# Second attention of a four-layer graph network: four row buffers, seven slots per period, ScalarE's passes and copies in a fixed alternation, results one period later

## The chip, the cores and the metric

The kernel runs on one core of one Trainium2 chip. A core has five engines that work side by side and wait for one another through semaphores: TensorE (matrix products; PE in the profile, PEld for its weight loads), VectorE (DVE), ScalarE (ACT), GpSimd (POOL) and SyncE (SP, which here only starts DMAs). Each engine takes its own instructions strictly in the order in which the program has them. The metric is device time in microseconds (us) of one execution.

## The reference

Four layers on 3327 nodes with 256 features, each `x = layernorm(x + layer(x, adj))`. Layer 0 averages over neighbours, layer 1 is a graph convolution with a state-space scan, layer 2 is graph attention, layer 3 is top-p attention with diffusion. The change touches layer 3, whose core is:

```python
def _top_p_attention(X, W1, W2, W3):
    q = X @ W1.T @ W2.T
    k = X @ W3.T
    probs = softmax(q @ k.T, axis=-1)
    idx = argsort(-probs, axis=-1)
    sp = take_along_axis(probs, idx, axis=-1)
    cs = cumsum(sp, axis=-1)
    keep_sorted = cs - sp < TOP_P            # 0.9
    ...
    A = probs * mask
    return A / maximum(A.sum(-1, keepdims=True), 1e-12)

R = (S + eye(N)); R = R / R.sum(-1, keepdims=True)
for n in range(2):
    A = _top_p_attention(Xa, W1, W2, W3)
    Xf = R @ Xf
    Xa = A @ Xa
    Z = Z + Xf @ U1[n].T + Xa @ U2[n].T
h = layernorm(X + Z)
```

In each of the two steps every row of the attention keeps the largest probabilities until their sum reaches 0.9. `S` is the adjacency.

## The kernel before

Rows are padded to 3328 and cut into 26 tiles (`nt`) of 128 rows. A tile's row of attention, `e`, is 128 x 3328 numbers. Layer 3 runs two stages over the tiles, the first attention (step 0, `p=0`) and the second attention (step 1, `p=1`), which is the last work of the kernel.

Helpers are Python generators: each `yield` is a point where the loop that drives them may go on to another one. The loop therefore writes down the order of work by hand, and a scheduler behind it orders each engine's instructions by readiness, except those wrapped in `keep_in_program_order` (`here`), which stay in the order in which the loop wrote them. For a tile of the second attention the helpers are:

- `scores` (L781): products of queries and keys in four groups of two 416-wide halves into one PSUM tile `sc`; ScalarE copies each group into `e` (L795, the last group in two pieces, L798).
- `search_long` (L903): finds the cut-off value of each row. `m8` (L913) takes a maximum of the first 416 columns. ScalarE then makes six passes over the whole of `e`: Exp of half the value for a sum (L917), Exp in place (L918), and, after VectorE has set a first threshold `c1` (L922 to L928), Relu and Sign about it (L929, L931). From these VectorE estimates a second threshold `c2` (L933 to L949), and ScalarE passes again (L950, L952). A third threshold `c3` (L965 to L974) cuts `e` into `z` (L977, 3328 wide), of whose 26 segments VectorE takes the top eight each (L853, MAX8), ranks them in six rounds (L864, L866) and finds the crossing `v` (L873 to L876). Ties are dropped by two MATCH_REPLACE8 (L1001), and the select L1008 clears everything under `v` and sums what is kept.
- `attended` (L830): seven groups of four transposes of `e` into PSUM (`tp`, four buffers), a copy of each group by ScalarE (`wt`, L839), four products each with `G` (L841).
- `diffused` (L814) and `aggregated` (L801): 26 products (L809) of the adjacency, loaded in chunks of `J3` = 7 tiles by SyncE (`at`, L807, three buffers), and the result `xf` (L827). It is made `DL` = 4 tiles ahead of the attention that uses it.
- `second` (L1049): two normalizations of the row (`h`, L1052, L1060, L1061; statistics L84, L85). GpSimd computes the inverse root (`power`, L593, L594), VectorE `nb` (L1068), ScalarE the last scaling (L1069), SyncE writes `out` (L1071).

The driving loop (L1146) has one round per tile i. It works on four things: the attention of tile i-1 (`values`), the search of tiles i and i+1, and the scores of tile i+2; the result of tile i-1 follows in the same round. `e` has three buffers (L1109), so the scores of tile i+2 go into the buffer from which tile i-1 has just been transposed.

`J3`, `DL`, the buffers of `e` and the helpers `diffused`, `aggregated` and `attended` are shared with the first attention.

Of the kernel before, what the change touches and what calls it, by code (L numbers as in the profile page):

```python
# [9 lines left out]
F32 = mybir.dt.float32  # L10
BF16 = mybir.dt.bfloat16
I32 = mybir.dt.int32
AF = mybir.ActivationFunctionType
# [24 lines left out]
J3 = 7  # L38
DL = 4
# [4 lines left out]
def gnn_kernel(ctx: ExitStack, tc: tile.TileContext, n: int, a: dict, out: bass.AP):  # L44
# [539 lines left out]
    with tc.tile_pool(name="l3", bufs=1) as pool, tc.tile_pool(name="l3d", bufs=1, space=DRAM) as dram:  # L584
# [195 lines left out]

        def scores(work, psum, p, q, e):  # L781

            if npad > n:
                nc.gpsimd.memset(e[:, n:], NEG)
            halves = e.rearrange("p (h c) -> p h c", h=2)
            for c0 in range(0, half, KC):
# [7 lines left out]
                if ws[0] == ws[1]:  # L794
                    nc.scalar.copy(halves[:, :, c0:c0 + ws[0]], pl[:, :, :ws[0]])  # L795
                else:
                    for h, w in enumerate(ws):
                        nc.scalar.copy(halves[:, h, c0:c0 + w], pl[:, h, :w])  # L798
                yield

        def aggregated(atp, psum, it, rhs):  # L801

            acc = psum.tile([P, D], F32, name="acc")
            for j0 in range(0, nt, J3):
# [6 lines left out]
                yield None  # L811
            yield acc

        def diffused(work, atp, psum, p, it, out):  # L814
# [8 lines left out]
            for acc in aggregated(atp, psum, it, Y if p else X):  # L823
                if acc is None:
                    yield
# [4 lines left out]
        def attended(work, psum, e, rhs, tp=2):  # L830

            acc = psum.tile([P, D], F32, name="acc")
            for j0 in range(0, nt, 4):
# [5 lines left out]
                nc.scalar.copy(wt[:, :m, :], pt[:, :m, :])  # L839
# [10 lines left out]
        def segment_tops(cand, z, lo=0, hi=nseg):  # L850

            for s in range(lo, hi):
                nc.vector.max(cand[:, s * 8:(s + 1) * 8], z[:, s * SEG:(s + 1) * SEG])  # L853
# [15 lines left out]
        def crossing(work, v, top, base, lim):  # L869

            k = top.shape[1]
            cs = work.tile([P, k], F32, name="cs")
            nc.vector.tensor_tensor_scan(cs, ones[:, :k], top, initial=base, op0=ALU.mult, op1=ALU.add)  # L873
            over = work.tile([P, k], F32, name="over")
# [26 lines left out]
        here = tc.keep_in_program_order  # L901

        def search_long(work, sm, e, total, v, kept, halves=False):  # L903
# [12 lines left out]
            junk = work.tile([P, npad], BF16, name="junk", bufs=1)  # L916
            nc.scalar.activation(junk, e, AF.Exp, bias=hneg, scale=0.5, accum_out=root)  # L917
            nc.scalar.activation(e, e, AF.Exp, bias=neg, accum_out=total)  # L918
# [9 lines left out]
            nc.vector.tensor_scalar_mul(nc1, c1, -1.0)  # L928
            here(nc.scalar.activation(junk, e, AF.Relu, bias=nc1, accum_out=f1))  # L929
# [19 lines left out]
            nc.vector.tensor_scalar_mul(nc2, c2, -1.0)  # L949
            here(nc.scalar.activation(junk, e, AF.Relu, bias=nc2, accum_out=f2))  # L950
            yield
            here(nc.scalar.activation(junk, e, AF.Sign, bias=c2, scale=-1.0, accum_out=sg))  # L952
# [11 lines left out]
            yield  # L964
            nc.vector.tensor_scalar(k2, sg, -0.5, npad / 2, op0=ALU.mult, op1=ALU.add)  # L965
# [10 lines left out]
            z = work.tile([P, npad], F32, name="z", bufs=1)  # L976
            nc.vector.scalar_tensor_tensor(z, e, c3, e, op0=ALU.is_lt, op1=ALU.mult, accum_out=rest)  # L977
            nc.vector.tensor_sub(base, total, rest)
            nc.vector.scalar_tensor_tensor(base, big, 1.0, base, op0=ALU.is_lt, op1=ALU.mult)
            cand = candidates(work)  # L980
            segment_tops(cand, z, 0, nseg // 2)
            yield
            segment_tops(cand, z, nseg // 2)
# [12 lines left out]
            for i, (r, c) in enumerate(((up, 0), (r, half))):  # L996
# [4 lines left out]
                nc.vector.match_replace(part[:, ::-1], drop, part[:, ::-1], 0.0)  # L1001
                if halves:
                    nc.vector.scalar_tensor_tensor(part, part, v, part, op0=ALU.is_ge, op1=ALU.mult,
                                                   accum_out=sums[:, i:i + 1])
            if halves:
# [12 lines left out]
        def first(work, psum, it, acc, f, xf):  # L1018

            xa = work.tile([P, D], F32, name="xa")  # L1020
# [28 lines left out]
        def second(work, psum, it, acc, f, xf):  # L1049
# [18 lines left out]
            nc.vector.scalar_tensor_tensor(nb, mv[:, 0:1], -1.0, rs, op0=ALU.mult, op1=ALU.mult)  # L1068
            nc.scalar.activation(h, h, AF.Identity, scale=rs, bias=nb)  # L1069
# [32 lines left out]
        with tc.tile_pool(name="l3w", bufs=2) as work, tc.tile_pool(name="l3s", bufs=4) as sm, \  # L1102
# [3 lines left out]
            def start(p, t, es, searches, search):  # L1106
                q = work.tile([2 * DA, P], F32, name="q")
                nc.sync.dma_start(q, qd[p][t])
                es[t] = work.tile([P, npad], F32, name="e", bufs=3)  # L1109
# [34 lines left out]
            with tc.tile_pool(name="l3q", bufs=2, space=PSUM) as psum:  # L1144
                es, searches, xfs = {}, {}, []
                for i in range(-2, nt + 1):  # L1146
# [4 lines left out]
                    values, result = iter(()), iter(())  # L1151
                    if 0 < i:
                        values = attended(work, psum, es[i - 1], G, tp=4)

                    def weigh(steps):
                        for _ in range(steps):
                            next(values, None)

                    weigh(3)
                    search(i + 1)  # L1160
                    search(i)
                    weigh(2)
                    search(i + 1)
                    weigh(2)
# [4 lines left out]
                    next(result, None)  # L1169
                    logits = start(1, i + 2, es, searches, search_long) if i + 2 < nt else iter(())  # L1170
                    more = range(len(xfs), min(nt, max(i, 0) + DL + 1))
                    spread = diffused(work, atp, psum, 1, more[0], xfs) if more else iter(())
                    next(logits, None)
                    next(logits, None)
                    next(spread, None)
                    search(i + 1)
                    both(logits)
                    next(spread, None)
                    search(i + 1)
                    search(i + 2)  # L1180
                    next(result, None)
                    both(spread)
                    search(i)
                    for _ in result:
                        pass
# [145 lines left out]
```

## Time and profile before

| | us |
|---|---|
| three timed runs | 3853.97, 3858.10, 3861.62 (median 3858.1) |
| the profiled execution | 3856.61 |
| its span, first to last instruction | 3854.7 |
| mean granted TensorE clock | 0.955 |
| busy: TensorE, VectorE, ScalarE, GpSimd | 3499.9, 2610.2, 1738.5, 494.7 |
| first product of the second attention's diffusion (L809) | 2912.7 |
| first `z` (L977), last `z` | 2950.5, 3800.0 |

Section 1 of the page gives busy time per engine with the share of the span; the window view gives the same for chosen stretches, with the clock that TensorE was granted (PEclk) and the share of the DMA engines; the list of waits says which instruction waited for which, with the total, the number of times and the longest; the timeline lists instructions in order with start and duration, and in brackets the idle time before one and what ended it. An `x8` behind a product of 256 columns means four products, since each is two records.

### The profile page before, as it was taken

To read this page: it belongs to the slowest core of one execution; us is meant where nothing else is said; L and a number is where in the kernel's file an instruction comes from. 1 tells how busy PE (TensorE), PEld (TensorE's weight loads), DVE (VectorE), ACT (ScalarE), POOL (GpSimd) and SP (SyncE) were. 2 spreads that over 40 slices of the span, in tenths; PEclk is the share of its full clock that TensorE was granted. 3 is DMA by queue.
4 is the path that set the end of the run, shared out by engine and by line. 5 is a ranking of instruction groups with operands and counts; after the bars stand their busy time and mean duration, and the time that the engine had idled before them with its cause. 6 is when DMAs were issued, how large, how long until landed. Compare 5 with 4: busy or idle time off the path is not lost. (4 is left out here: it accounts for less than half of the span.)

```text
span 3854.7 us, 41751 instructions
## 1 busy us (share of the span) xinstructions
PE 3499.9 (91%) x15079; PEld 2593.0 (67%) x15079; DVE 2610.2 (68%) x5588; ACT 1738.5 (45%) x2612; POOL 494.7 (13%) x734
## 2 busy tenths in 40 slices
PE   8999999898889778689989999999999999999975
PEld 7888876554554434378868787777777667667664
DVE  1111579898988999877753445444454888888987
ACT  0000665554545465211122333333346777777773
POOL 0000122222221221111110000000001111111110
PEclk9999999998999888889999999999999999999997
DMA  7443211111111000044423222122203112221100
GB/s 231 139 134 95 84 59 53 37 46 36 42 36 36 6 0 0 15 158 139 148 73 88 62 61 56 51 59 62 59 11 101 58 56 63 64 63 54 58 23 7
DMA packets 100529, 252.96 MB, mean 66 GB/s; under 512 B 14786, under 2 KB 49090, under 8 KB 100178
## 3 DMA queue, kind: packets, MB, share of 16 engines
q1 hardware_dynamic: 100306, 250.13, 21.2%
q8 instruction: 122, 2.00, 0.2%
q14 instruction: 101, 0.83, 0.1%
HBM read 239.86 MB, written 10.22 MB: 65 GB/s over the span
## 5 line engine op out<-in xcount | busy, mean ns | idle before, releaser
L473 DVE TENSOR_TENSOR_SCAN h<-dA,db 128x2052 f32<-128x2052 f32 (+3 forms) x128 | 464.0, 3625 | 5.9 <-PE y L557 3.4
L460 ACT ACTIVATE dA<-dt,A_log 128x512 f32<-128x512 f32 (+3 forms) x512 | 297.0, 637 | 326.7 <-DVE h L473 272.7
L557 PE MATMUL y<-h,ident 128*128 128x512 f32 (+3 forms) x1024 | 436.1, 563 | 3.2 <-DVE h L549 3.2
L841 PE MATMUL acc<-G,wt 128*128 128x256 f32 x1352 | 332.7, 396 | 63.4 <-ACT wt L839 62.2
L557 PEld LDWEIGHTS y<-h,ident 128*128 128x128 f32 x1024 | 199.4, 207 | 258.0 <-issue 232.4
L839 ACT COPY wt<-tp 128x512 f32<-128x512 f32 (+1 forms) x364 | 185.9, 554 | 382.7 <-PE tp L837 382.4
L841 PE MATMUL acc<-X,wt 128*128 128x256 f32 x1352 | 343.8, 391 | 10.3 <-ACT wt L839 9.8
L841 PEld LDWEIGHTS acc<-G,wt 128*128 128x128 f32 x1352 | 254.1, 194 | 133.7 <-ACT wt L839 81.6
L809 PE MATMUL acc<-F,at 128*128 128x256 f32 x1352 | 323.1, 389 | 0.6 <-ACT q L604 0.6
L116 PE MATMUL acc<-xa,at 128*128 128x257 f32 x1352 | 310.1, 383 | 5.4 <-DMA at<-in_adjT 5.4
L841 PEld LDWEIGHTS acc<-X,wt 128*128 128x128 f32 x1352 | 242.3, 189 | 105.5 <-issue 41.3
L732 PE MATMUL acc<-F,at 128*128 128x257 f32 x1352 | 307.9, 384 | 4.9 <-DVE at L729 4.9
L264 PE MATMUL cb<-F,at 128*128 128x256 f32 x1352 | 310.6, 382 | 1.6 <-ACT hn L283 1.6
L809 PE MATMUL acc<-X,at 128*128 128x256 f32 x1352 | 309.4, 383 | 2.9 <-issue 2.9
L809 PEld LDWEIGHTS acc<-F,at 128*128 128x128 f32 x1352 | 253.8, 193 | 74.0 <-issue 40.0
L264 PEld LDWEIGHTS cb<-F,at 128*128 128x128 f32 x1352 | 257.3, 191 | 58.7 <-issue 17.7
L466 DVE TENSOR_TENSOR db<-du,row 128x2048 f32<-128x2048 f32 (+3 forms) x128 | 240.2, 1879 | 82.6 <-ACT row L448 82.5
L853 DVE MAX8 cand<-e 128x8 f32<-128x128 f32 x676 | 142.2, 281 | 226.4 <-ACT e L795 214.9
L116 PEld LDWEIGHTS acc<-xa,at 128*128 128x128 f32 x1352 | 256.7, 192 | 42.6 <-issue 5.4
L809 PEld LDWEIGHTS acc<-X,at 128*128 128x128 f32 x1352 | 255.0, 192 | 44.0 <-issue 10.9
L732 PEld LDWEIGHTS acc<-F,at 128*128 128x128 f32 x1352 | 256.4, 193 | 41.8 <-issue 5.1
L549 DVE TENSOR_TENSOR h<-h,C 128x2048 f32<-128x2048 f32 (+3 forms) x128 | 240.9, 1882 | 37.2 <-PE C L484 23.7
(305 smaller groups left out, 5303.6 us busy)
## 6 DMA issues: line engine op xcount, KB each, us to landing
at<-in_adjT SPq DMA_DIRECT2D x102, 832.0 KB, 4.5
at<-in_adjT SPq DMA_DIRECT2D x156, 448.0 KB, 3.4
at<-in_adjT SPq DMA_DIRECT2D x52, 576.0 KB, 3.8
at<-in_adjT SPq DMA_DIRECT2D x52, 320.0 KB, 3.0
at<-in_adjT SPq DMA_DIRECT2D x26, 512.0 KB, 3.5
xt<-in_xT SPq DMA_DIRECT2D x26, 128.0 KB, 4.1
qd<-q SPq DMA_DIRECT2D x104, 32.0 KB, 1.9
q<-qd SPq DMA_DIRECT2D x52, 64.0 KB, 2.3
```

The lines of the kernel that those rows point to most:

```text
L116: nc.tensor.matmul(acc, at[:, j, :], rhs[:, j0 + j, :], start=(j0 + j == 0), stop=(j0 + j == nt - 1))
L264: nc.tensor.matmul(acc, at[:, j % JC, :], X0[:, j, :], start=(j == 0), stop=(j == nt - 1))
L460: nc.scalar.activation(dA[:, g, 1:], dt[:, g, :], AF.Exp, scale=A[:, g, s:s + 1])
L466: nc.vector.tensor_mul(by_group(dbs[s % 2], w)[:, :, 1:], du, B.to_broadcast([P, NG, w]))
L473: nc.vector.tensor_tensor_scan(h[:, :m], dAs[s % 2][:, :m], dbs[s % 2][:, :m], initial=0.0, op0=ALU.mult, op1=ALU.add)
L549: nc.vector.tensor_mul(h, h, C.to_broadcast([P, NG, w]))
L557: nc.tensor.matmul(ys[g][:, :w], ident, h[:, g, :], start=False, stop=(s == DS - 1))
L732: nc.tensor.matmul(acc, at[:, j, :], F[:, j0 + j, :], start=(j0 + j == 0), stop=(j0 + j == nt - 1))
L809: nc.tensor.matmul(acc, at[:, j, :], rhs[:, j0 + j, :], start=(j0 + j == 0), stop=(j0 + j == nt - 1))
L839: nc.scalar.copy(wt[:, :m, :], pt[:, :m, :])
L841: nc.tensor.matmul(acc, wt[:, j, :], rhs[:, j0 + j, :], start=(j0 + j == 0), stop=(j0 + j == nt - 1))
L853: nc.vector.max(cand[:, s * 8:(s + 1) * 8], z[:, s * SEG:(s + 1) * SEG])
```

## The change

It rewrites the loop of the second attention and where the helpers yield.

- `e` gets four buffers. The round is written as seven slots, each with some diffused products, one group of transposes with its copy and products, and one step of a search. Scores of tile i+2 are spread over the round, one group at a time.
- `search_long` yields around every one of its six passes, and after the second threshold. All its passes, the copies of `scores` and of `attended` and the last scaling of `second` are kept in program order on ScalarE: in a steady round score copy, transpose copy, Exp, score copy, transpose copy, last scaling, score copy, transpose copy, Relu, score copies, transpose copy, Sign, transpose copy, half Exp, transpose copy, second Relu, transpose copy, second Sign.
- `issue_after(bound[0].ins)` puts the two MATCH_REPLACE8 of a tile behind the second threshold of the next.
- `z` is made in two halves of 1664 in one buffer, and its two sums are put together by one more small operation.
- The result of tile i-1 is written in round i+1 instead of round i. `nb` is computed on GpSimd.
- `J3` goes from 7 to 5, `DL` from 4 to 2, `tp` from four buffers to three in the second attention, the PSUM pool's other tiles from two to three; some small tiles lose their second buffer to make room.

```diff
-J3 = 7
-DL = 4
+J3 = 5
+DL = 2
...
+        def in_order(op):
+            return lambda *x, **k: tc.keep_in_program_order(op(*x, **k))
+
         def scores(work, psum, p, q, e):
+            copy = in_order(nc.scalar.copy) if p else nc.scalar.copy
...
-                    nc.scalar.copy(halves[:, :, c0:c0 + ws[0]], pl[:, :, :ws[0]])
+                    copy(halves[:, :, c0:c0 + ws[0]], pl[:, :, :ws[0]])
...
-        def aggregated(atp, psum, it, rhs):
+        def aggregated(atp, psum, it, rhs, each=J3):
...
-                yield None
+                    if (j0 + j) % each == each - 1 or j0 + j == nt - 1:
+                        yield None
...
-        def attended(work, psum, e, rhs, tp=2):
+        def attended(work, psum, e, rhs, tp=2, copy=nc.scalar.copy):
...
-            junk = work.tile([P, npad], BF16, name="junk", bufs=1)
-            nc.scalar.activation(junk, e, AF.Exp, bias=hneg, scale=0.5, accum_out=root)
-            nc.scalar.activation(e, e, AF.Exp, bias=neg, accum_out=total)
+            junk = junks[0] = junks[0] or work.tile([P, npad], BF16, name="junk", bufs=1)
+            yield
+            here(nc.scalar.activation(junk, e, AF.Exp, bias=hneg, scale=0.5, accum_out=root))
+            yield
+            here(nc.scalar.activation(e, e, AF.Exp, bias=neg, accum_out=total))
             yield
...
-            nc.vector.tensor_scalar_mul(nc2, c2, -1.0)
-            here(nc.scalar.activation(junk, e, AF.Relu, bias=nc2, accum_out=f2))
-            yield
-            here(nc.scalar.activation(junk, e, AF.Sign, bias=c2, scale=-1.0, accum_out=sg))
+            bound[0] = nc.vector.tensor_scalar_mul(nc2, c2, -1.0)
...
+            yield
+            here(nc.scalar.activation(junk, e, AF.Relu, bias=nc2, accum_out=f2))
+            yield
+            here(nc.scalar.activation(junk, e, AF.Sign, bias=c2, scale=-1.0, accum_out=sg))
...
-            z = work.tile([P, npad], F32, name="z", bufs=1)
-            nc.vector.scalar_tensor_tensor(z, e, c3, e, op0=ALU.is_lt, op1=ALU.mult, accum_out=rest)
-            nc.vector.tensor_sub(base, total, rest)
+            cand = candidates(work)
+            for h, r in enumerate((rest, base)):
+                part = e[:, h * half:(h + 1) * half]
+                z = work.tile([P, half], F32, name="z", bufs=1)
+                nc.vector.scalar_tensor_tensor(z, part, c3, part, op0=ALU.is_lt, op1=ALU.mult, accum_out=r)
+                yield
+                segment_tops(cand[:, h * half // SEG * 8:], z, half // SEG)
+                yield
+            nc.vector.tensor_scalar(base, base, rest, total, op0=ALU.add, op1=ALU.subtract)
             nc.vector.scalar_tensor_tensor(base, big, 1.0, base, op0=ALU.is_lt, op1=ALU.mult)
+            nc.vector.tensor_scalar_mul(base, base, -1.0)
...
-                nc.vector.match_replace(part[:, ::-1], drop, part[:, ::-1], 0.0)
+                with tc.issue_after(bound[0].ins):
+                    nc.vector.match_replace(part[:, ::-1], drop, part[:, ::-1], 0.0)
...
-            nc.vector.scalar_tensor_tensor(nb, mv[:, 0:1], -1.0, rs, op0=ALU.mult, op1=ALU.mult)
-            nc.scalar.activation(h, h, AF.Identity, scale=rs, bias=nb)
+            nc.gpsimd.tensor_scalar(nb, mv[:, 0:1], rs, -1.0, op0=ALU.mult, op1=ALU.mult)
+            here(nc.scalar.activation(h, h, AF.Identity, scale=rs, bias=nb))
...
-                es[t] = work.tile([P, npad], F32, name="e", bufs=3)
+                es[t] = work.tile([P, npad], F32, name="e", bufs=4)
...
+                    def slot(products, looks, pair=False):
+                        if pair:
+                            next(logits, None)
+                        for _ in range(products):
+                            next(spread, None)
+                        next(values, None)
+                        search(looks)
+
+                    search(i)
+                    slot(3, i + 1, True)
+                    next(result, None)
+                    search(i)
+                    search(i + 1)
+                    search(i)
+                    next(logits, None)
+                    next(result, None)
+                    search(i + 2)
+                    for _ in range(3):
+                        next(spread, None)
+                    next(values, None)
+                    search(i)
+                    for _ in result:
+                        pass
+                    slot(3, i + 1, True)
+                    slot(3, i + 1, True)
+                    both(logits)
+                    search(i)
+                    slot(5, i + 2)
+                    search(i + 1)
+                    search(i)
+                    slot(5, i + 1)
+                    slot(4, i + 1)
+                    both(spread)
+                    search(i)
                     if 0 < i:
                         f = normalizer(sm, kepts[1][:, i - 1:i], tots[1][:, i - 1:i])
                         result = second(work, psum, i - 1, next(values), f, xfs[i - 1])
```

The text names instructions by their lines before the change. After it the same instructions stand lower: L853 becomes L858, L917 L926, L918 L928, L929 L940, L931 L942, L949 L960, L950 L973, L952 L975, L965 L977, L977 L992, L1001 L1017, L1008 L1025, L1061 L1078, L1068 L1085, L1069 L1086; copies that go through `in_order` (L795, L798, L839) stand under its line L782.

## The prediction

> **What bounds the kernel now.** I read the engine totals first, then the stage that the change touches, then who waits there.
>
> ```profile
> PE 3499.9 (91%) x15079; PEld 2593.0 (67%) x15079; DVE 2610.2 (68%) x5588; ACT 1738.5 (45%) x2612; POOL 494.7 (13%) x734
> ```
>
> TensorE is busy for 91% of the span, but that is an average over stages. The second attention runs from about 2912 us to the end at 3854.7. I put its 26 tiles on a clock by the start of L977 (`z`, once per tile): tile 0 at 2950.5, tile 1 at 2978.6, tile 2 at 3017.9, tile 23 at 3739.6, tile 24 at 3769.9, tile 25 at 3800.0. From tile 5 to tile 22 the distances alternate between 36.2 and 32.1, so a pair takes 68.3 and a tile 34.15. The window view shows such a pair, and a late tile that has no neighbour products left:
>
> ```profile
> core 0: us, PE busy (x) PEld busy (x) DVE busy (x) ACT busy (x) POOL busy (x), PEclk, DMA share, GB/s
> 3361.70:3397.90 36.20, 32.10 (x160) 24.52 (x158) 29.94 (x114) 24.01 (x24) 4.39 (x8) 1.00 0.23 72
> 3397.90:3430.00 32.10, 30.33 (x135) 23.47 (x136) 30.13 (x114) 27.50 (x28) 4.38 (x8) 0.95 0.17 51
> 3739.60:3769.90 30.30, 15.53 (x67) 10.88 (x66) 29.17 (x113) 25.39 (x24) 2.42 (x6) 0.77 0.01 5
> ```
>
> VectorE is busy for 30 us in each, whether the period is long or short. TensorE needs a mean of 31.2, ScalarE 25.8. The last row matters most: with half of TensorE's work gone, the period still takes 30.3. VectorE is the floor; what differs between periods is waiting. The waits of the same pair:
>
> ```profile
> PE acc L841 <- ACT wt L839: 5.8, 3, 3.6
> ...
> DVE k L965 <- ACT junk L952: 3.7, 1, 3.7
> ACT junk L950 <- DVE s L959: 3.1, 1, 3.1
> ...
> DVE nb L1068 <- POOL rs L594: 1.7, 2, 1.1
> DVE h L1061 <- POOL rs L594: 1.4, 2, 0.8
> ```
>
> In the long period ScalarE waits 3.1 us for the second threshold (L949, L959), then VectorE waits 3.7 us for the two passes over it (L950, L952). The timeline of VectorE shows why:
>
> ```profile
> 3389.00 0.15 DVE L949 TENSOR_SCALAR nc<-c 128x1 f32<-128x1 f32 x1
> ...
> 3392.08 0.16 DVE L1068 SCALAR_TENSOR_TENSOR nb<-mv,rs 128x1 f32<-128x1 f32 x1 [1.05 <-POOL rs L594]
> 3395.99 0.15 DVE L965 TENSOR_SCALAR k<-sg 128x1 f32<-128x1 f32 x1 [3.74 <-ACT junk L952]
> ```
>
> The threshold is a few tiny instructions, but they stand behind two MATCH_REPLACE8 (1.88 each) and the 3.68 us select L1008. When it is out at 3389.0, VectorE has only 3 us of other work left.
>
> **The change, part by part.** (Line numbers are those before the change throughout.)
>
> *The order of the threshold.* `issue_after(bound)` and the slots put threshold 2 of tile i+1 ahead of the two MATCH_REPLACE8 and the select of tile i. Behind it VectorE then has 2 x 1.9 + 3.7 + about 3.2 of normalization = 10.8 us. ScalarE needs after it: L950 3.2, one short copy 0.4, L952 3.2 = 6.8. The 3.7 us wait goes, with 4 us of margin. What is late next is VectorE itself.
>
> *VectorE's period, summed.* I start from the short period, which has no ScalarE wait: 32.1 = 30.1 busy + 1.4 POOL waits + 0.6 of dependence gaps. Changes: `nb` moves to GpSimd, which takes its instruction and its 0.6 us wait (-0.7); the 0.8 wait for `rs` before L1061 stays. `z` in two halves: L1003, also 1664 wide, takes 1.95 against 3.68 for 3328, so two cost 2 x 1.87 - 3.61 in pitch (+0.13). One more [P,1] operation on `base` (+0.1). The threshold chain stands alone instead of interleaved with the ranking: at tile 0 it ran alone, 2939.20 to 2941.18, 2.0 us, against about 1.3 of pure issue (+0.7). The crossing loses partners too (+0.2). **Sum: 32.5 us.**
>
> *TensorE's period.* 52 products at 0.425 (32 records of L809 take 6.8 us, two per product) = 22.1; 26 transposes at 0.126 = 3.3; 4 score groups at 0.9 plus 0.2 for the switch = 4.4; together 29.8. I walk it from the first transpose (0), which waits for the select. The one real stall is the next tile's first score group: its PSUM tile is freed by the fourth score copy, behind L929, which waits for threshold 1 (6.9 us after `z` starts, at 12.9 of the walk), so the copy ends at 17.1 where TensorE arrives at 15.6. With this 1.5 a round ends at 31.4, 1.1 inside 32.5. `tp` falls from four buffers to three, and each copy stands just before a pass: in the walk a copy never comes over 0.3 us after TensorE wants it, since three diffused products (1.3) cover each round trip.
>
> *ScalarE.* Six passes at 3.2, seven transpose copies at 0.5, four score copies, one normalization: 27 us, 5.5 us slack. On the same walk: L929 from 13.0 to 16.2, score copies to 17.1, transpose copy 17.6, L931 20.8, a copy that waits for its transposes 21.9, L917 25.1, the next likewise 26.2, L950 29.4, copy 29.8, L952 33.0, that is 27 us after the start of its period's `z` (5.9 on the walk); VectorE asks for it at 30.0. Its fixed order is the new risk (rival D).
>
> *A rule on the clock.* After the 3.6 us gap behind the copies, eight records of L841 took 2.58 us; without such a gap 1.99:
>
> ```profile
> 3399.67 2.58 PE L841 MATMUL acc<-G,wt 128*128 128x256 f32 x8 [3.58 <-ACT wt L839]
> 3302.97 1.99 PE L841 MATMUL acc<-G,wt 128*128 128x256 f32 x8 [1.00 <-ACT wt L839]
> ```
>
> The Trainium skill ("TensorE: Matmul & The Clock Gate", The HAM clock gate) says that about 3.4 us without work halve TensorE's clock until it has been busy that long again. By the row the penalty is 0.6 us in the short periods (granted 0.95); by the rule up to 1.7. The rule speaks against one part: with DL 2 the ramp has two tiles fewer of diffused products (2 x 26 x 0.425 = 22 us) between tile 0's scores and its first transpose, so TensorE idles and starts it cold. By row +0.6, by rule +1.7, once: VectorE bounds there, so I take 0. In the steady slots my longest gap is 1.5, so both say no penalty.
>
> *A rule on `nb`.* GpSimd rows alone and beside a select:
>
> ```profile
> 3322.93 0.22 POOL L593 TENSOR_SCALAR rs<-mv 128x1 f32<-128x1 f32 x1
> 3820.49 1.95 DVE L1003 SCALAR_TENSOR_TENSOR e<-e,v 128x1664 f32<-128x1664 f32 x1
> 3820.63 1.89 POOL L593 TENSOR_SCALAR rs<-mv 128x1 f32<-128x1 f32 x1 [3.09 <-DVE drop L998]
> ```
>
> The skill ("SBUF — State Buffer", Who interferes with whom) says that a VectorE instruction with two SBUF inputs locks a GpSimd one that reads SBUF out for its whole length, which speaks against moving work there. By the free row `nb` costs 0.22, by the rule up to 1.9 beside the first half of `z`, where I place it. Then L1069 on ScalarE starts at about 8.0 of the walk instead of 6.4. Behind it stand the third score copy, the third transpose copy and L929, which waits for threshold 1 until 12.9: either value is hidden. I take 0; without that cover it would be 1.9 x 23 = 44 us.
>
> *Chunks of 5 products instead of 7.* Six transfers per tile instead of four. The page has 320 KB landing in 3.0 us, 448 KB in 3.4. With three buffers a chunk is asked for two chunks ahead, 4.3 us of pure products: still more than 3.0. On SyncE's queue they stand behind `out` (waits for L1069, about 8.5 of the walk) and the query load; the fifth chunk, next behind these, is wanted at about 24.7. Nothing is paid.
>
> *Four row buffers.* Scores of tile i+2 no longer wait until tile i-1 is transposed, so their copies spread over the period instead of standing in a block. This makes the alternation possible; alone I cost it at 0.
>
> *Ramp and tail.* Tile 0: before its second Relu, ScalarE now also has tile 1's first pass (3.2) and an earlier score copy (0.85): `z` at 2954.6 instead of 2950.5. Tile 1 follows by 29 (before 28.1), at 2983.6. Tile 2, still without a result to normalize, by 30.5: 3014.1; before, this took 39.3. Then 21 periods of 32.5: tile 23 at 3696.6. The last two, with tiles missing, 32.0 and 31.5: tile 25 at 3760.1 (before 3800.0). Diffused work is over two tiles later, but VectorE bounds those periods. From there 54.7 to the end, less 2 for a normalization that now falls behind the last select: 3812.8. The first attention shares DL, J3 and the buffers; TensorE is 99% busy there, work is the same, and its last periods (47.2 and 48.0 busy of 50) get two more tiles of cover: -1. Span 3811.8, plus 1.9 around it (3856.61 - 3854.7) = 3813.7. I add 0.2 per period for jitter between engines now within 1 us of each other (+4.6). The profiled run is 1.5 under the median of 3858.1, inside its scatter. **Forecast: 3818 us.**
>
> **Rivals.**
> - A, the forecast: periods of 32.3 to 33.0, 3808 to 3828. For it: the short periods already run at 32.1.
> - B, VectorE packs tighter: 30.3 without TensorE load shows that the dependence gaps can be filled. At 31.4: 1.3 x 22 less, 3789. Against: the new chain stands alone.
> - C, TensorE becomes the bound through hand-offs: seven transposes, each needing a copy between two passes, lose 0.3 us more each: 31.4 + 2.1 = 33.5; 23 x 0.8 more, about 3838 to 3842. For it: 1.1 us is little slack, and PE's waits for `wt` are today's largest.
> - D, slower: ScalarE's fixed order closes a loop. From threshold 1 it runs L929, score copies, L931, L917, L950, L952 with four transpose copies between, 20 us in my walk, then VectorE's third threshold (2.6) and `z` to the next threshold 1 (6.9): 29.9 with signals. It decides from 32.5, and makes the kernel slower from about 34.3. If three copies each come one group of four products (1.7) later, it is 35.0: 3818 + 2.5 x 23 = 3875. Against it: TensorE has diffused products, not products waiting for copies, ahead of each transpose.
> - The change having no effect would need the 3.7 us wait to survive; the fixed order forbids it.
>
> **Numbers.** A 0.57, B 0.15, C 0.20, D 0.08. About 0.2% (7.7 us) is what a measurement here can tell from no change; C's upper end (0.03) and D's lower (0.01) lie within it. Faster 0.89, same 0.04, slower 0.07. Range 3795 to 3846: B's nearer half to beyond C.
>
> **What would show it.** Distances of `z` even, near 32.5, where 36.2 and 32.1 alternated; no wait of L965 (`k`) for L952; no wait of VectorE for `nb`; granted clock near 1.00 in the stage; ScalarE waiting about 5 us per period, mostly before L929 and the copies. Wrong if the distances still alternate, if TensorE's wait for `wt` keeps 3 us per period, or if L929 starts when ScalarE is free rather than on threshold 1.

## The result and the profile after

The changed kernel takes 3811.95 us (median of four runs, 3810.20 to 3813.87) where the kernel before, run beside it, takes 3856.41 (four runs): a ratio of 0.9883, 95% interval 0.9866 to 0.9900. The profiled execution took 3813.28 us, its span is 3811.5. The forecast was 3818. (From here on, lines of the changed kernel carry its own numbers; the list at the end of the section on the change translates them.)

The engine totals are nearly the old ones; they don't tell what happened:

```profile
PE 3482.6 (91%) x15079; PEld 2570.3 (67%) x15079; DVE 2626.2 (69%) x5640; ACT 1739.7 (46%) x2612; POOL 497.9 (13%) x760
```

The clock by the first `z` of each tile (L992) does. Tile 0 starts at 2951.3, tile 1 at 2979.2, tile 2 at 3009.5, tile 3 at 3039.0; from tile 4 (3071.4) to tile 22 (3661.2) every distance is 32.7 or 32.8; tile 23 is at 3693.8, tile 25 at 3754.8. The alternation of 36.2 and 32.1 is gone. Of the 43.2 us by which the span is shorter, 16.7 are gained from tile 0 to tile 4 (136.8 before, 120.1 now) and 29.4 from there to tile 25; the stretch behind the last `z` takes 2.0 longer, and tile 0 comes 0.8 later. The window view of two neighbouring periods and of the last but one tile:

```profile
3399.10:3431.90 32.80, 30.27 (x147) 22.86 (x146) 31.09 (x116) 25.89 (x25) 4.67 (x10) 1.00 0.22 63
3431.90:3464.70 32.80, 30.26 (x147) 22.86 (x146) 31.10 (x116) 25.88 (x25) 4.67 (x10) 1.00 0.21 62
...
3725.90:3754.80 28.90, 16.91 (x67) 13.22 (x66) 27.98 (x111) 16.38 (x16) 1.87 (x5) 0.75 0.01 5
```

The columns are those of the windows shown before: VectorE (third pair) is busy for 31.1 of 32.8, TensorE for 30.3 at a granted clock of 1.00, ScalarE for 25.9. The list of waits for these two periods together:

```profile
ACT wt L782 <- PE tp L842: 8.3, 6, 2.6
...
ACT junk L940 <- DVE nc L938: 3.2, 2, 1.6
...
PE sc L797 <- ACT e L782: 2.8, 2, 1.4
...
PE tp L842 <- DVE e L1025: 2.3, 2, 1.1
...
DVE h L1078 <- POOL rs L594: 1.5, 2, 0.8
```

VectorE waits once in a period, 0.77 us for GpSimd's `rs`. It no longer waits for the second Sign pass. TensorE's products no longer wait for a transpose copy (5.8 us in the pair before); only weight loads still do, 0.6 us at most, beside running products. Nothing that VectorE needs comes late by ScalarE's waits. VectorE's timeline shows the new order around the second threshold (L960) and at the end of the period:

```profile
3417.63 0.15 DVE L960 TENSOR_SCALAR nc<-c 128x1 f32<-128x1 f32 x1
...
3417.84 1.88 DVE L1017 MATCH_REPLACE8 e<-drop,e 128x1664 f32<-128x1664 f32 x1
...
3428.39 0.49 DVE L1078 SCALAR_TENSOR_TENSOR h<-h,rs,t 128x256 f32<-128x256 f32 x1 [0.77 <-POOL rs L594]
3428.79 0.15 DVE L977 TENSOR_SCALAR k<-sg 128x1 f32<-128x1 f32 x1
...
3430.14 0.63 DVE L980 TENSOR_TENSOR s<-s,dm 128x1 f32<-128x1 f32 x1
```

L977, the successor of the old L965 that waited 3.74 us, starts without a bracket: ScalarE's two passes over the threshold have long ended (at 3425.69).

### The profile page after: what moved, and what is told of

Read it like the earlier page. It is cut to its first block, busy times and chain, and to the rows that moved or that the text cites. A ratio compares the mean times of both kernels' runs of the same rounds, so it can differ in the third digit from the quotient of the medians.

```text
span 3811.5 us, 42006 instructions
## 1 busy us (share of the span) xinstructions
PE 3482.6 (91%) x15079; PEld 2570.3 (67%) x15079; DVE 2626.2 (69%) x5640; ACT 1739.7 (46%) x2612; POOL 497.9 (13%) x760
## 5 line engine op out<-in xcount | busy, mean ns | idle before, releaser
L846 PE MATMUL acc<-G,wt 128*128 128x256 f32 x1352 | 345.7, 397 | 11.7 <-ACT wt L782 11.2
L846 PE MATMUL acc<-X,wt 128*128 128x256 f32 x1352 | 343.6, 391 | 8.3 <-ACT wt L844 8.0
L813 PE MATMUL acc<-F,at 128*128 128x256 f32 x1352 | 339.3, 380 | 1.7 <-ACT q L604 0.6
L846 PEld LDWEIGHTS acc<-G,wt 128*128 128x128 f32 x1352 | 247.2, 193 | 112.3 <-ACT wt L782 46.2
L846 PEld LDWEIGHTS acc<-X,wt 128*128 128x128 f32 x1352 | 242.5, 189 | 103.2 <-issue 41.3
L858 DVE MAX8 cand<-e 128x8 f32<-128x128 f32 x676 | 142.1, 278 | 226.2 <-ACT e L799 214.6
L732 PEld LDWEIGHTS acc<-F,at 128*128 128x128 f32 x1352 | 255.9, 192 | 41.6 <-issue 5.2
L813 PEld LDWEIGHTS acc<-X,at 128*128 128x128 f32 x1352 | 253.7, 191 | 43.2 <-issue 10.2
L813 PEld LDWEIGHTS acc<-F,at 128*128 128x128 f32 x1352 | 243.2, 190 | 39.2 <-issue 7.8
L797 PE MATMUL sc<-kT,q 64*128 64x416 f32 x832 | 201.5, 561 | 37.7 <-ACT e L782 34.3
```

What stands on the lines that cost most here:

```text
L732: nc.tensor.matmul(acc, at[:, j, :], F[:, j0 + j, :], start=(j0 + j == 0), stop=(j0 + j == nt - 1))
L797: nc.tensor.matmul(pl[:, h, :w], q[k, :], kT[p][k, c0:c0 + w], start=True, stop=True)
L813: nc.tensor.matmul(acc, at[:, j, :], rhs[:, j0 + j, :], start=(j0 + j == 0), stop=(j0 + j == nt - 1))
L846: nc.tensor.matmul(acc, wt[:, j, :], rhs[:, j0 + j, :], start=(j0 + j == 0), stop=(j0 + j == nt - 1))
```

## The experiments

Each kernel ran beside the kernel before. "Mean distance" is that of `z` from tile 5 to tile 22, 17 periods.

| run | what it is | median us | ratio to before (95%) | mean distance |
|---|---|---|---|---|
| before | | 3853 to 3856 | 1 | 34.05 |
| after | | 3811.95 | 0.9883 (0.9866 to 0.9900) | 32.77 |
| a_noorder | after, no edge at MATCH_REPLACE8 | 3841.56 | 0.9962 (0.9951 to 0.9972) | 34.38 |
| b_order | before, with that edge | 3885.67 | 1.0088 (1.0066 to 1.0109) | 35.86 |
| b_osign | b_order, Sign earlier | 3837.05 | 0.9953 (0.9934 to 0.9971) | 33.39 |
| b_min | b_osign, `nb` on GpSimd | 3830.17 | 0.9934 (0.9921 to 0.9948) | 33.04 |
| a_copies | after, copies not pinned | 3811.92 | 0.9892 (0.9874 to 0.9910) | 32.78 |
| b_jd | before, J3 = 5 and DL = 2 | 3848.01 | 0.9984 (0.9978 to 0.9991) | 34.29 |
| a_nb | after, `nb` on VectorE | 3828.56 | 0.9934 (0.9917 to 0.9950) | 33.65 |
| a_pe_less | after, 5 products fewer per tile | 3799.17 | 0.9857 (0.9843 to 0.9872) | 32.29 |
| a_dve_less | after, no MATCH_REPLACE8 | 8733.61 | 2.2676 (2.2643 to 2.2709) | 30.83 |
| a_fill2 | after, `rs` wait filled | 3788.65 | 0.9832 (0.9820 to 0.9845) | 31.71 |
| a_gps | after, GpSimd's sums moved | 3814.77 | 0.9895 (0.9875 to 0.9914) | 33.08 |
| a_tail | a_fill2, last tile's halves in turn | 3789.25 | 0.9829 (0.9809 to 0.9849) | 31.71 |

### Where the threshold stands

First theory: the edge that holds the two MATCH_REPLACE8 behind the next tile's second threshold carries the gain. Its rival: the slots and ScalarE's fixed order carry it. The edge was taken out of the changed kernel, and put alone into the kernel before. a_noorder:

```diff
-                with tc.issue_after(bound[0].ins):
-                    nc.vector.match_replace(part[:, ::-1], drop, part[:, ::-1], 0.0)
+                nc.vector.match_replace(part[:, ::-1], drop, part[:, ::-1], 0.0)
```

> The changed kernel without the edge that holds the two MATCH_REPLACE8 behind the next tile's second threshold; slots, four row buffers and ScalarE's fixed order stay. Theory 1 (threshold's place): distances alternate again, with a mean of 33.8 to 34.3, VectorE waits 3 to 4 us for the second Sign pass in every other period, time 3840 to 3855. Theory 2 (slots and fixed order carry the gain): mean distance at most 33.0, time at most 3820.

The alternation is back, 36.5 to 37.4 and 32.1 to 32.5, and 30 of the 44 us are lost. The time is the first theory's, the mean just above its range, but the wait that appears is another than expected. VectorE's timeline of a long period (lines up to L1015 as in the changed kernel, from there one less):

```profile
3370.37 3.67 DVE L1024 SCALAR_TENSOR_TENSOR e<-e,v 128x3328 f32<-128x3328 f32 x1
...
3374.80 0.15 DVE L960 TENSOR_SCALAR nc<-c 128x1 f32<-128x1 f32 x1
3379.69 0.48 DVE L1068 SCALAR_TENSOR_TENSOR h<-acc,f,xf 128x256 f32<-128x256 f32 x1 [3.89 <-PE acc L846]
```

The threshold comes out behind the select, ScalarE's L973 waits 5.92 us for it, and with the fixed order a transpose copy stands behind L973: TensorE gets it late, and VectorE waits 3.89 us for TensorE's result, not for a pass. A late threshold costs VectorE the same, by a longer way.

b_order puts the same edge, and nothing else, into the kernel before:

> The kernel before, with the two MATCH_REPLACE8 held behind the next tile's second threshold and nothing else. Theory 1 (the place of the second threshold on VectorE is what cost the long periods): distances of z become even, 32.3 to 33.5, VectorE's 3.7 us wait for L952 is gone, time 3812 to 3832. Theory 2 (the fixed alternation on ScalarE and the spread scores carry the gain, the threshold's place is only part of it): TensorE's wait for wt stays near 3 us per period and sets the pace, distances 33.7 or more in the mean, time 3845 or more.

The second theory's bounds hold (33.7 or more, 3845 or more, TensorE's wait of 3 us per period), but neither theory said that the kernel would be slower than before, and it is, by 0.9%. The order on VectorE is as wanted in every period, but the distances are 36.5 and 35.2. The waits of two such periods, and three lines of ScalarE's and VectorE's timelines in one of them (line numbers of this kernel are one or two higher than those before the change):

```profile
ACT wt L839 <- PE tp L837: 10.9, 2, 6.1
...
DVE k L934 <- ACT junk L932: 3.5, 2, 2.4
```

```profile
3415.78 0.59 ACT L839 COPY wt<-tp 128x512 f32<-128x512 f32 x1 [6.10 <-PE tp L837]
3416.26 3.07 ACT L932 ACTIVATE junk<-e,c 128x3328 bf16<-128x3328 f32 x1
```

```profile
3419.45 0.15 DVE L934 TENSOR_SCALAR k<-sg 128x1 f32<-128x1 f32 x1 [2.40 <-ACT junk L932]
```

ScalarE has the fifth transpose copy ahead of the first Sign pass. The copy waits for TensorE, Sign stands behind it, and the new edge makes VectorE wait for the threshold that Sign feeds, where it used to go on with MATCH_REPLACE8. The old order, bad as it was, had covered this. The two waits for Sign, 3.5 us in two periods, only take the place of the old 3.7, though. What comes on top is that the second threshold's chain of small operations now stands alone: from the first ranking MAX8 to the first MATCH_REPLACE8 VectorE needs 10.0 us without the wait, where the short period before had 8.7. b_osign tests what Sign's place is worth by moving Sign's step ahead in the loop of b_order:

```diff
-                    weigh(2)
                     search(i + 1)
-                    weigh(2)
+                    weigh(4)
```

> The kernel before with the two MATCH_REPLACE8 held behind the next tile's second threshold, as in b_order, and the step of the first Sign pass (L931 of the kernel before) moved ahead of the next two groups of transposes, so that it no longer stands behind the fifth transpose copy on ScalarE. Theory (b_order is slow because that copy, which waits 4.8 to 6.1 us for TensorE, holds Sign up, and VectorE waits 1.1 and 2.4 us for it): that wait goes, distances of z fall from 35.85 to 34.5 or less, time 3855 or less. Rival (TensorE's wait of 3.0 us for its first copy behind two Exp passes, and the slow products after it, set the pace): distances stay at 35.3 or more, time 3870 or more.

As the theory has it, and further: 48.6 us less than b_order, 19 less than before, with two small edits and none of the slots. TensorE's hand-offs are not cured: in every second period it still waits 3.84 us for its first copy, and the granted clock is 0.96 over four periods. b_min adds `nb` on GpSimd (the edit of a_nb, the other way round):

> The kernel before with three of its edits only: the two MATCH_REPLACE8 behind the next tile's second threshold, the first Sign's step ahead of the next two groups of transposes (both as in b_osign), and nb on GpSimd. No slots, no fourth row buffer, J3 and DL as before. Theory 1 (VectorE sets the pace of b_osign too, so nb is worth there what it is in the changed kernel, 0.85 us per period): mean distance of z 32.4 to 32.7, time 3814 to 3824. Theory 2 (TensorE's hand-offs, whose wait for the first transpose copy is 3.8 us there and makes its next products slow, set the pace, so the slots are needed for the rest): mean distance 33.1 or more, time 3831 or more.

Between the two, nearer the second: the wait for TensorE's first copy is still 3.25 us in every second period. So three small edits bring 25 of the 44 us; the rest of the change (slots, fourth row buffer, shorter chunks and what goes with them) brings another 18 between these two kernels. Half of that is no matter of the steady periods: the changed kernel is 9.4 us shorter from tile 0 to tile 4 (120.1 against 129.5), and only 4.6 from tile 5 to tile 22. In the steady periods TensorE's supply differs, with that wait and a clock of 0.96 here, no wait for a copy and 1.00 in the changed kernel. VectorE itself waits here, in four periods (3345.5 to 3478.1), 2.9 us for score copies (`m`, L914) and 2.4 for the Exp in place (`lim`, L884), and in the changed kernel for neither. Which part of the rest brings which share was not tested.

### Parts that cost or bring little

a_copies leaves ScalarE's passes in program order but frees the copies:

```diff
-            copy = in_order(nc.scalar.copy) if p else nc.scalar.copy
+            copy = nc.scalar.copy
...
-                        values = attended(work, psum, es[i - 1], G, 3, in_order(nc.scalar.copy))
+                        values = attended(work, psum, es[i - 1], G, 3)
```

> The changed kernel with the score copies and transpose copies of the second attention free for the scheduler to place; the six passes keep their order. Theory 1 (threshold's place, VectorE is the bound): distances of z stay within 0.2 of 32.75, time within 6 us of 3812. Theory 2 (the alternation of passes and copies carries the gain): copies gather between passes again, TensorE waits for wt about 3 us per period, distances 33.5 or more, time 3830 or more.

Nothing changes, as VectorE's bound has it. But the scheduler chose nearly the same alternation from the slots (one score copy goes ahead of a transpose copy), so this shows that the pinning isn't needed, not that the alternation isn't.

b_jd takes `J3 = 5` and `DL = 2` into the kernel before:

> The kernel before with J3 = 5 and DL = 2 alone. The prediction (nothing is paid for chunks of five, the shorter lead costs nothing in steady periods, the first attention gains 1): time within 6 us of 3856, distances alternating at 36.2 and 32.1. Rival (transfers come late or the ramp starves): waits of L809 for at, time 3864 or more; other rival (the lead of four was itself a cost): 3848 or less.

The alternation stays, no new wait comes, and the gain of 0.16% (0.09 to 0.22) is at the edge of what counts; the median stands at the bound of the second rival (3848), 2 us outside the first range. It comes from the first tiles: tile 2 follows tile 1 by 30.8 instead of 39.3, and of these 8.5 us tile 3 loses 3.2 again (36.4 instead of 33.2).

What was not tried: three row buffers in the changed kernel (the slots write the scores of tile i+2 while tile i-1 is still being transposed, so the order needs the fourth), and `z` in one piece or chunks of seven there.

### What a step on VectorE is worth

a_nb moves `nb` back:

```diff
-            nc.gpsimd.tensor_scalar(nb, mv[:, 0:1], rs, -1.0, op0=ALU.mult, op1=ALU.mult)
+            nc.vector.scalar_tensor_tensor(nb, mv[:, 0:1], -1.0, rs, op0=ALU.mult, op1=ALU.mult)
```

> The changed kernel with nb back on VectorE. The prediction's sum (VectorE is the bound, and nb with its wait costs it 0.7 us per period): distances of z 33.3 to 33.6, a wait of VectorE for rs before nb of 0.3 to 1.1, time 3824 to 3831. Rival (VectorE's order has other work to put into that wait, so only the instruction's pitch of about 0.1 us counts): distances 32.8 to 33.0, time 3812 to 3818.

The sum holds: 0.88 us per period and 16.6 in the time (19.7 by the two ratios to the kernel before). VectorE's timeline shows where:

```profile
3407.95 0.16 DVE L1085 SCALAR_TENSOR_TENSOR nb<-mv,rs 128x1 f32<-128x1 f32 x1 [0.79 <-POOL rs L594]
```

a_pe_less takes work from TensorE instead. It leaves out 5 of the 26 diffused products of a tile (so the diffusion's sum lacks five blocks of neighbours):

```diff
-                    nc.tensor.matmul(acc, at[:, j, :], rhs[:, j0 + j, :],
-                                     start=(j0 + j == 0), stop=(j0 + j == nt - 1))
+                    if each > 1 or j % 5 != 4:
+                        nc.tensor.matmul(acc, at[:, j, :], rhs[:, j0 + j, :],
+                                         start=(j0 + j == 0), stop=(j0 + j == nt - 1))
```

> The changed kernel with 5 of the 26 diffused products of each tile of the second attention left out (21 remain), 2.1 us of TensorE per tile. If VectorE is the bound: distances of z stay at 32.6 to 32.9, time within 6 us of 3812. Rival (TensorE and its hand-offs are the bound): distances fall by 1 to 2, to 30.8 to 31.8, time 3770 to 3790.

Both numbers missed; the bound is VectorE's all the same. Of 2.1 us less on TensorE 0.48 show in the period. The timeline gives it to VectorE's own order, which the scheduler chose anew: in three periods of four (32.5) the operations ahead of the first MATCH_REPLACE8 stand closer (9.0 us from the first ranking MAX8, 9.3 in the changed kernel), as the `drop` operations and the threshold's chain are mixed there; in the fourth (31.8) the first operation of the third threshold falls into the wait for `rs`, and L981 (L980 before this edit) takes 0.12 us instead of 0.63. VectorE's only wait is still that for `rs`. That pointed to a_fill2, below.

a_dve_less takes work from VectorE: both MATCH_REPLACE8, so that ties at the cut-off stay. The kernel's fallback for unresolved rows then runs behind the stage, so ties do occur in this data; the time is that of the fallback, and only the distances say something of the stage.

> The changed kernel with both MATCH_REPLACE8 of each tile of the second attention left out, so ties at the cut-off are not dropped (3.7 us of VectorE per tile); the select is held behind the threshold instead. The prediction's walk (TensorE stands next, at 31.4 with its stall at the score group): distances fall to 31.2 to 31.7, not to 29.1, time 3775 to 3787. Rival 1 (hand-offs vanish with VectorE's time, only TensorE's 30.3 of work is left): distances 30.3 to 30.8, time 3755 to 3768. Rival 2 (TensorE is the bound already): distances 32.5 or more.

```profile
3369.20:3400.00 30.80, 30.15 (x147) 22.91 (x147) 27.48 (x111) 25.65 (x27) 4.62 (x10) 1.00 0.22 67
```

At 30.83 the period is TensorE's: it is busy for 30.15, VectorE for 27.5, and VectorE waits 1.5 us per period for TensorE's result (L846). That is just above the first rival's 30.3 to 30.8, and below the 31.2 that the prediction's walk asked for. So TensorE's wall stands 1.9 us under the changed kernel's period, and its stall at the score group shrinks as VectorE gets faster, from 1.4 to 0.6.

### VectorE's gaps, and a faster kernel

In a_fill2 the second step of the normalization is held behind the third operation of the third threshold:

```diff
-            nc.vector.tensor_sub(dm, m1, m2)
+            late[0] = nc.vector.tensor_sub(dm, m1, m2)
...
-            nc.vector.scalar_tensor_tensor(h, h, rs, xb, op0=ALU.mult, op1=ALU.add)
+            with tc.issue_after(late[0].ins) if after else nullcontext():
+                nc.vector.scalar_tensor_tensor(h, h, rs, xb, op0=ALU.mult, op1=ALU.add)
```

> The changed kernel with the second step of the normalization (L1078, which waits 0.77 us for GpSimd's rs) held behind the first operations of the third threshold, so that these fill the wait. If VectorE is the bound and every gap of it counts: distances of z fall by 0.5 to 0.9, to 31.9 to 32.3, time 3791 to 3801. Rival (the later L1078 delays the last scaling and with it the score copies, TensorE follows): distances 32.6 or more, time 3808 or more.

It beats both kernels and its own forecast: 1.06 us per period and 23 us in the time (20 by the two ratios to the kernel before), more than the wait of 0.77. Its VectorE timeline (L1079 is L1078 of the changed kernel):

```profile
3414.60 0.15 DVE L984 SCALAR_TENSOR_TENSOR c<-c,m 128x1 f32<-128x1 f32 x1
3414.96 0.48 DVE L1079 SCALAR_TENSOR_TENSOR h<-h,rs,t 128x256 f32<-128x256 f32 x1 [0.21 <-POOL rs L594]
3415.36 0.15 DVE L980 TENSOR_TENSOR s<-s,dm 128x1 f32<-128x1 f32 x1
```

The wait falls by 0.56, and L980 from 0.63 to 0.15: 1.04 together. L980 has 128 elements in and out; beside it, in the changed kernel, GpSimd made a sum of 128x256, in GpSimd's timeline:

```profile
3430.01 0.75 POOL L827 TENSOR_TENSOR t<-t,s 128x256 f32<-128x256 f32 x1
```

a_gps tests that: the other sum (with the bias) gets a buffer of its own and goes behind `nb`, so that L823 and L827 come earlier.

```diff
-            xb = work.tile([P, D], F32, name="t")
-            nc.gpsimd.tensor_tensor(xb, X[:, it, :], b3, op=ALU.add)
+            xb = work.tile([P, D], F32, name="xb", bufs=1)
+            with tc.issue_after(nbs[0].ins) if after and nbs[0] else nullcontext():
+                nc.gpsimd.tensor_tensor(xb, X[:, it, :], b3, op=ALU.add)
```

> The changed kernel with GpSimd's two operations for the diffusion (L823, L827 of it) moved away from VectorE's third threshold: the sum with the bias gets a buffer of its own and is made behind nb. VectorE's order is the same. Theory (L980 takes 0.63 us instead of 0.15 because GpSimd adds beside it, and VectorE is the bound): L980 falls to 0.2 or less, distances fall by 0.3 to 0.5, to 32.3 to 32.5, time 3800 to 3807. Rival (the two then stand beside the select, are held back until its end and delay rs, so that VectorE waits longer before L1078): distances 32.7 or more, time 3809 or more.

L980 falls to 0.15, as the theory says, but the period grows to 33.08. It does not grow by a longer wait for `rs` (0.77 still): the same delay strikes elsewhere. VectorE's and GpSimd's timelines (from L1072 on one line lower than in the changed kernel):

```profile
3426.47 0.98 DVE L1078 SCALAR_TENSOR_TENSOR h<-h,mv,ln_g 128x256 f32<-128x256 f32 x1
...
3430.98 0.51 DVE L986 SCALAR_TENSOR_TENSOR c<-c,c,big 128x1 f32<-128x1 f32 x1
```

```profile
3426.44 0.73 POOL L827 TENSOR_TENSOR t<-t,s 128x256 f32<-128x256 f32 x1
...
3430.75 0.73 POOL L1072 TENSOR_TENSOR xb<-X,ln_b 128x256 f32<-128x256 f32 x1
```

Each of GpSimd's sums starts just ahead of a VectorE instruction with two inputs, which then takes 0.50 and 0.29 more than its 0.48 and 0.22 in the changed kernel: together 0.79 for the 0.48 saved at L980, which is the 0.31 by which the period grew. The rival's bounds are met (32.7, 3809), but by this and not by the wait that it named.

a_tail asks why the stretch from the last `z` to the end grew. In the last tile alone, the second MATCH_REPLACE8 is held behind the select of the first half:

```diff
-                with tc.issue_after(bound[0].ins):
+                with tc.issue_after((cut[0] if halves and i else bound[0]).ins):
```

> a_fill2 with, in the last tile alone, the second MATCH_REPLACE8 held behind the select of the first half. Theory (in the changed kernel the last tile's first transposes come 24.0 us after its z, before the change 22.6, because the first half's select stands behind the second MATCH_REPLACE8): they come at 22.3 to 22.8 and the stretch from the last z to the end falls from 56.7 to 54.5 to 55.5; time 3784 to 3790. Rival (TensorE starts cold there and takes back what it gains): the stretch stays at 56 or more. The periods stay at 31.7 in either.

The first transposes come 22.4 us after `z` (23.9 in a_fill2), and the stretch to the end is 55.2 (56.0): 1.5 gained, 0.6 given back, too little to show in the time. The products behind those transposes, a_tail above and a_fill2 below:

```profile
3755.54 5.76 PE L846 MATMUL acc<-G,wt 128*128 128x256 f32 x16
```

```profile
3756.49 5.15 PE L846 MATMUL acc<-G,wt 128*128 128x256 f32 x16
```

## Why the prediction was right, point by point

**VectorE as the floor, and the threshold's place.** Right. a_nb and a_fill2 turn 0.9 and 1.1 us of VectorE into 17 and 23 us of time, 2.1 us of TensorE bring 0.48 per period, by another order on VectorE. The threshold's place is worth most of the gain: without the edge 30 us come back, as a wait of 3.9 us in the long periods. What the prediction did not see is that the edge needs the rest. It said that ScalarE needs 6.8 us after the threshold and has 10.8; in the changed kernel the passes end 8.1 us after it (3417.63 to 3425.69), because ScalarE is still busy and then waits for a transpose, and VectorE asks for them after 11.2, so that the margin is 3 and not 4. What stands ahead of the feeding passes it did not look at, and by itself the edge costs 30 us (b_order). One reading was loose: between tile 5 and tile 22 one distance before is 33.0, and the mean 34.05, not 34.15.

**VectorE's period.** 32.5 foreseen, 32.77 measured, by terms of the wrong size that nearly cancel. The short period before and one after, cut at the same instructions:

| stretch of VectorE | before | after | moved into it or out of it |
|---|---|---|---|
| `z` to the first ranking MAX8 | 10.20 | 9.34 | out: L827 of before (0.4) |
| to the first MATCH_REPLACE8 | 8.66 | 9.33 | out: `m8` and its two followers (0.6) |
| to the end of the select | 7.72 | 7.53 | out: first step of the normalization (0.4) |
| to the next `z` | 5.50 | 6.58 | in: these three (1.5); out: `nb` and its wait (0.9) |

The lone threshold and crossing cost 1.3 (8.66 to 9.33, with 0.6 moved out), where the prediction had 0.7 and 0.2. `nb` brings 0.88, not 0.7. The first stretch gets shorter by 0.46 beyond what left it: L923 took 0.53 there and L979 0.35, after the change (L933, L997) 0.15 and 0.14. And L980 costs 0.48 more beside GpSimd. L923 and L980 are one matter, which the prediction's sum does not have: GpSimd's sum, which had stood beside L923, moved to the end of the period (see the last section). With 32.7 or 32.8 in every steady period there is no jitter: the 4.6 us added for it are most of the 6 by which the forecast is high.

**TensorE.** The stall at the score group was put at 1.5 and is 1.39; the longest gap is that one, and the clock is 1.00 in every steady window, as foreseen. The wall of 31.4 was too high: without MATCH_REPLACE8 the period is 30.83, so slack was 1.9, not 1.1, and rival C weaker than its 0.20. (C's own terms, 23 periods of 0.8 on top of 3818, give 3836, not 3838 to 3842.) **ScalarE** waits 6.8 us per period rather than 5, L940 for threshold 1 as foreseen (1.6); D's loop shows nowhere.

**`nb` and its cover.** It took 0.28, as it began before `z`. The cover was needed and held in a_fill2: there GpSimd's L594 lay beside `z` and took 2.14 us instead of 0.56, and the last scaling began 2.8 us after `z` instead of 0.1, at no cost.

**Chunks and the shorter lead.** Put at nothing; b_jd gives 6 us, all at the start, where tile 2 follows tile 1 by 30.8. The prediction had that gain in its 30.5 for tile 2 (30.3 measured) without naming this cause; whether the chunks or the lead make it is not shown. What was mis-sized in the ramp stands earlier: the second tile's first pass falls partly into the 1.4 us for which ScalarE had waited for tile 0's threshold, and tile 1 follows by 27.9 instead of 29. `z` of tile 2 is 4.6 earlier than foreseen. The 1 us for the first attention can't be told: its end lies between 2905 and 2913 in these runs.

**Tail.** Foreseen 52.7, measured 56.7: the failed term is "less 2 for a normalization". Most of that normalization (L1069 to L1078, 3769.22 to 3772.40) still stands ahead of the last tile's MATCH_REPLACE8. Of the other 2.0 us, 1.4 come from the two selects of the last tile, which now stand behind both MATCH_REPLACE8 instead of alternating with them, so that the first transposes come 24.0 after `z` instead of 22.6; most of the rest are the products behind these (5.69 instead of 5.22). Start and end cancel: tile 2 is 4.6 early (1 of it the first attention's, as foreseen in the sum), the periods to tile 23 take 1.8 more than foreseen, the last two 2.5 less, the end 4.0 more. The sum for the span was 3811.8, and it is 3811.5; that is luck, closer than its parts deserve.

## What to carry to other kernels

When one engine fills a period, as VectorE does here, an operation or a wait on it is worth about its length times the number of periods, and a wait for a slow neighbour is cheap to fill with a chain that is ready anyway: one order edge brought 20 to 23 us here. An edge that holds one queue back moves the wait to whatever feeds it: before adding it, read what stands ahead of the feeding instruction on its own engine, as b_order shows. And a sum that comes out right can do so by parts that cancel, so compare it stretch by stretch.

## What the hardware showed beyond that

*GpSimd delays VectorE too.* A VectorE instruction with two inputs of 128x1 (L980) takes 0.63 instead of 0.15 us when a GpSimd sum of 128x256 (0.75) has begun just ahead of it, in 17 of 17 periods; when the sum is moved, the delay moves (0.98 and 0.51 in a_gps). What the small instruction loses is what is left of the sum: in each of these periods L980 ends 0.01 to 0.03 us after L827, and so does L986 behind its sum in a_gps (0.51) and in a_fill2 (0.39 instead of 0.22). The kernel before had it too, in its short periods, beside the sum L822 (3403.12 to 3403.85):

```profile
3403.33 0.53 DVE L923 TENSOR_TENSOR c<-c,tot 128x1 f32<-128x1 f32 x1
```

The prediction had used only the other direction (0.22 to 1.89 for L593 beside a select; in a_fill2 L594 takes 2.14 instead of 0.56 beside `z`). The Trainium skill ("SBUF — State Buffer", Who interferes with whom) has both: "Issue order, not op shape, decides who blocks." The 128x1 rows agree. The 128x256 one (0.98) does so only in part: it lost 0.50 where 0.70 of the sum was left.

*The same gap, two prices.* In b_order TensorE's 32 products came twice behind a wait of nearly the same length (its timeline):

```profile
3369.90 8.86 PE L841 MATMUL acc<-G,wt 128*128 128x256 f32 x32 [3.05 <-ACT wt L839]
...
3405.06 10.19 PE L841 MATMUL acc<-G,wt 128*128 128x256 f32 x32 [3.02 <-ACT wt L839]
```

The window view has the granted clock at about half for 3.1 us after the first, and for 5.9 after the second:

```profile
3369.90:3373.00 3.10, 3.10 (x8) 2.51 (x9) 3.10 (x17) 3.05 (x3) 0.35 (x1) 0.55 0.15 48
3373.00:3376.00 3.00, 3.00 (x13) 2.54 (x13) 2.90 (x15) 1.51 (x3) 0.00 (x0) 0.89 0.00 0
...
3405.10:3408.00 2.90, 2.90 (x7) 2.36 (x8) 2.90 (x16) 2.84 (x3) 0.31 (x1) 0.50 0.14 45
3408.00:3411.00 3.00, 3.00 (x8) 2.37 (x8) 2.90 (x15) 1.68 (x3) 0.00 (x0) 0.50 0.00 0
```

So a gap just over 3 us costs 1.3 us more one time than the other; in b_min two waits of 3.24 and 3.25 us are followed by 9.98 and 8.86 for the same 32 records. That is what the Trainium skill's free-running window ("TensorE: Matmul & The Clock Gate", The HAM clock gate) would give; no run here varies the phase on purpose. Counted from the last product the gap is longer: 1.9 us of transposes lie ahead of the 3.0, and whether these count as work is not shown.
